# Loads in the order of need: keys' weights in halves, second attention's weights behind feed-forward chunks

## The chip, the cores and the metric

The kernel runs on one core of one Trainium2 chip. A core has a matrix engine (TensorE, PE in the profile), a vector engine (VectorE, DVE), an activation engine (ScalarE, ACT), a general engine (GpSimd, POOL) and a queue engine (SyncE, SP) that here only issues transfers. Data moves between the chip's memory and the core's SBUF by 16 DMA engines. The metric is the device time of one execution in microseconds, as the median of some runs.

## The reference, cut to what matters

Two layers, each a gated cross-attention and a gated feed-forward, over x of 2 x 2048 rows of 512 and a context of 2 x 128 rows of 384.

```
x = x + tanh(g_xattn[0]) * cross_attention_0(layernorm(x), ctx)     # 16 heads of 32, with biases
x = x + tanh(g_ffn[0])   * routed_block(layernorm(x))               # 256 rows of 2048 per batch:
                                                                    # causal attention, gated feed-forward 1365
x = x + tanh(g_xattn[1]) * cross_attention_1(layernorm(x), ctx)     # 16 heads of 64, inner width 1024
x = x + tanh(g_ffn[1])   * quantized_feed_forward(layernorm(x))     # 512 -> 2048, conv, silu, -> 512
```

A cross-attention needs keys = ctx @ Wk, values = ctx @ Wv, queries = x @ Wq, softmax over the 128 context rows, and an output projection with Wo and bo. The routed block scores all rows of a batch, takes the 256 highest, runs attention and a feed-forward on them and writes them back. The two matrices of the last feed-forward are first reduced to the values -1, 0, 1 (`ternary`).

## The kernel before, in words

Rows are worked in blocks of 512, four tiles of 128 rows by 512. The work has these stages.

- Opening (lines 986 to 1001): the weights of the first attention are loaded, the keys and values of the context computed (`keys_values`, line 176), and block 0 of x normalized, transposed and projected to queries (`front` and `queries` in `cross_attention`).
- First cross-attention, with the router and the first batch's selected attention fed in between its units (`beside`).
- First feed-forward on the selected rows of batch 0 (`feed_forward(0, ...)`, line 1033), with the rest of the router and the reduction of the second quantized matrix (`ternary(1, ...)`) in between.
- Selected attention of batch 1 with the second attention's keys and values in between (lines 1042 to 1061).
- Second feed-forward, batch 1 (line 1065), with `ternary(0, ...)` in between.
- Second cross-attention and the quantized feed-forward (from line 1077).

In names of the profile, `L_` stands for both `L0_` and `L1_`: L_ctxT, L_wk, L_wv, L_wq, L_wo, L_bo, L_bk, L_bq, L_bv are the context and the weights and biases of a cross-attention, L_kT and L_v its keys and values in SBUF. `pk` and `pv` are the PSUM tiles of keys and values (two buffers together in the opening), `xn` is a normalized tile of x, `ptr` its transpose, `pq` the queries. In the feed-forward, `w1c`, `w2c` and `w3c` are the weights of one chunk of 128 of the 1365 hidden columns (11 chunks, numbered 0 to 10, the last one of 85; three buffers each, loaded three chunks ahead), `pu` and `pw` the two up-projections, `gT` their gated product, `acc` the down-projection. `hn` is a normalized selected row tile, `wv` and `wqk` the selected attention's weights, `w_d` the quantized second matrix in memory, `w2b` its tile in SBUF, `xf` the x tiles of the second cross-attention.

A scheduler places every instruction on its engine. It keeps each engine's own order, adds the waits for data and for memory that is used again, and may move an instruction ahead of others that were written earlier if it is ready sooner. Each engine, and so each queue of transfers, then runs its instructions strictly in that order: an instruction that waits holds up all behind it. Nearly all transfers are issued on SP; in the opening ACT issues six and GpSimd two. In the built program each transfer on SP or ACT takes one of eight completion counters in turn, and waits until the transfer that had the counter before it has landed.

The weights of one attention are loaded by two methods. `load_context` issues the context, Wk, Wq, Wv and bv; `load_rest` issues Wo and bo and multiplies bo by the gate on VectorE. In the opening both are called at once. For the second attention `load_context` stands after the first feed-forward in the text and `load_rest` in the third step of the selected attention; the scheduler issues the first of them while the first feed-forward still loads its last chunks.

Of the kernel before, what the change touches and what calls it, by code (L numbers as in the profile page):

```python
# [17 lines left out]
P = 128  # L18
# [12 lines left out]
NF = (DFF + P - 1) // P  # L31
# [7 lines left out]
def row_tiles(ap):  # L39
    return ap.rearrange("(c p) n -> p c n", p=P)  # L40
# [3 lines left out]
def flamingo_kernel(ctx: ExitStack, tc: tile.TileContext, a: dict, out: bass.AP):  # L44
    nc = tc.nc
# [4 lines left out]
    def psum_pool(stack, name, bufs):  # L50
        return stack.enter_context(tc.tile_pool(name=name, bufs=bufs, space=PSUM))
# [23 lines left out]
    def in_pool(pool, tag):  # L75
        return lambda shape, name: pool.tile(shape, F32, name=name, tag=tag)
# [62 lines left out]
    class CrossWeights:  # L139


        def __init__(self, L, nE, bias, g, st, side):
            self.L, self.nE, self.bias, self.g = L, nE, bias, g
            E = nE * P
            w = st.enter_context(tc.tile_pool(name=L + "w", bufs=1, side=side))
            self.wq = w.tile([P, DC, E], F32, name=L + "wq")
            self.wo = w.tile([P, nE, D], F32, name=L + "wo")
            self.bo = w.tile([P, D], F32, name=L + "bo")
            self.kT = w.tile([P, B, nE, M], F32, name=L + "kT")
# [2 lines left out]
                self.bq = w.tile([P, nE], F32, name=L + "bq")  # L152
                self.bk = w.tile([P, nE], F32, name=L + "bk")

        def load_context(self, st, side):

            L, E = self.L, self.nE * P
            wkv = st.enter_context(tc.tile_pool(name=L + "wkv", bufs=1, side=side))
            self.ctxT = wkv.tile([P, CC, B * M], F32, name=L + "ctxT")
            nc.sync.dma_start(out=self.ctxT, in_=row_tiles(a["ctxT"]))  # L160
            self.wk = wkv.tile([P, CC, E], F32, name=L + "wk")
            nc.sync.dma_start(out=self.wk, in_=row_tiles(a[L + "WkT"]))
            nc.sync.dma_start(out=self.wq, in_=row_tiles(a[L + "WqT"]))
            self.wv = wkv.tile([P, CC, E], F32, name=L + "wv")
            nc.sync.dma_start(out=self.wv, in_=row_tiles(a[L + "WvT"]))
            if self.bias:
                self.bv = wkv.tile([P, E], F32, name=L + "bv")
                nc.sync.dma_start(out=self.bv, in_=a[L + "bv"].partition_broadcast(P))

        def load_rest(self):  # L170
            L = self.L
            nc.sync.dma_start(out=self.wo, in_=row_tiles(a[L + "WoT"]))
            nc.sync.dma_start(out=self.bo, in_=a[L + "bo"].partition_broadcast(P))
            nc.vector.tensor_scalar(self.bo, self.bo, self.g, None, ALU.mult)
# [432 lines left out]
        yield from rms_rows(rows, g2, h2T[b], mm, pool)  # L607

    AHEAD = 3

    def feed_forward(b, ps_acc, mm, work):

        w13, gT = {}, {}
        acc = [ps_acc.tile([P, D], F32, name=f"acc{i}", tag=f"acc{i}") for i in range(2)]

        def load(f):
            n = min(P, DFF - f * P)
            w1c = wst.tile([P, DC, P], F32, name="w1c", tag="w1c")
            nc.sync.dma_start(
                out=w1c[:, :, :n], in_=row_tiles(a["W1T"])[:, :, ds(f * P, n)]  # L620
            )
            w2c = wst.tile([P, DC, P], F32, name="w2c", tag="w2c")
            nc.sync.dma_start(
                out=w2c[:, :, :n], in_=row_tiles(a["W2T"])[:, :, ds(f * P, n)]
            )
            w3c = wst.tile([P, D], F32, name="w3c", tag="w3c")
            nc.sync.dma_start(out=w3c[:n, :], in_=a["W3T"][ds(f * P, n), :])
            w13[f] = (w1c, w2c, w3c)

        def down(f):  # L630
            n = min(P, DFF - f * P)
            for i in range(2):
                nc.tensor.matmul(
                    acc[i],
                    gT[f][:n, ts(i, P)],
                    w13[f][2][:n, :],
                    start=(f == 0),
                    stop=(f == NF - 1),
                )

        for f in range(AHEAD):
            load(f)
        for f in range(NF):
            n = min(P, DFF - f * P)
            pu, pw = mm([P, CAP], "pu"), mm([P, CAP], "pw")
            for pt, wt in ((pu, w13[f][0]), (pw, w13[f][1])):
                for d in range(DC):
                    nc.tensor.matmul(
                        pt[:n, :],
                        wt[:, d, :n],  # L650
                        h2T[b][:, d, :],
                        start=(d == 0),
                        stop=(d == DC - 1),
                    )
            su = fact.tile([P, CAP], F32, name="su", tag="su")
            nc.scalar.activation(su[:n, :], pu[:n, :], AF.Silu)
            gT[f] = fact.tile([P, CAP], F32, name="gT", tag="gT")
            nc.vector.tensor_tensor(gT[f][:n, :], pw[:n, :], su[:n, :], ALU.mult)
            if f > 0:
                down(f - 1)  # L660
                if f - 1 + AHEAD < NF:
                    load(f - 1 + AHEAD)
            for w, n in work:
                for _ in range(n):
                    next(w, None)
        down(NF - 1)
        for w, _ in work:
            for _ in w:
                pass

        for i in range(2):
            t = xa[2 * b + i]
            nc.vector.tensor_tensor(t, acc[i], t, ALU.add)
            nc.vector.tensor_scalar(t, t, gf[0], None, ALU.mult)
            nc.gpsimd.indirect_dma_start(
                out=x_d[b][:, :],
                out_offset=bass.IndirectOffsetOnAxis(
                    ap=idx[:, 2 * b + i : 2 * b + i + 1], axis=0
                ),
                in_=t,  # L680
                in_offset=None,
                compute_op=ALU.add,
            )
# [61 lines left out]
    with ExitStack() as st:  # L745
# [16 lines left out]
            out=pick,  # L762
            in_=pick,
# [10 lines left out]
            out=after,  # L774
            in_=after,
# [7 lines left out]
        def load_x(n, queue=nc.sync):  # L783
            if n < B * NBLK:
                for t in range(n * TB, (n + 1) * TB):
                    x[t] = xres.tile([P, D], F32, name="x", tag="x")
                    queue.dma_start(out=x[t], in_=x_in[t])
# [198 lines left out]
        sel_pools = selected_pools(st)  # L986
        W0 = CrossWeights("L0_", D // P, True, gx[0], st, "left")
        nc.scalar.dma_start(out=W0.bk, in_=a["L0_bk"])
        load_x(0, nc.scalar)
        nc.scalar.dma_start(out=W0.bq, in_=a["L0_bq"])  # L990
        with ExitStack() as st0:
            W0.load_context(st0, "left")
            W0.load_rest()
            nc.sync.dma_start(out=w_router, in_=a["w_router"].partition_broadcast(P))
            nc.vector.tensor_reduce(w_sum, w_router, AX.X, ALU.add)
            for n in (1, 2):
                load_x(n)
            selected_constants()
            with ExitStack() as st1:
                for _ in W0.keys_values(in_pool(psum_pool(st1, "L0_ps0", 2), "kv")):  # L1000
                    pass
# [18 lines left out]
    sf = ExitStack()  # L1020
    wst = sf.enter_context(tc.tile_pool(name="wst", bufs=AHEAD))
    fact = sf.enter_context(tc.tile_pool(name="act_ffn", bufs=3))
# [19 lines left out]
    right, right1, right2 = ExitStack(), ExitStack(), ExitStack()  # L1042
    w4 = right.enter_context(tc.tile_pool(name="w4", bufs=1, side="right"))
    w1q = w4.tile([P, DC, HID], BF16, name="w1q")
    W1 = CrossWeights("L1_", 1024 // P, False, gx[1], right1, "right")
    W1.load_context(right2, "right")
    with ExitStack() as sp:
        ps_o = psum_pool(sp, "s2b_o", 2)
        ps_sc = psum_pool(sp, "s2b_sc", 4)
        mm = in_pool(psum_pool(sp, "s2b_mm", 2), "mm")  # L1050
        second = selected_attention(
            1, mm, in_pool(ps_sc, "sc"), in_pool(ps_o, "o"), 4, selected_pools(sp), 2
        )
        keys_values = W1.keys_values(mm)
        for k, _ in enumerate(second):
            if k == 2:
                W1.load_rest()
            if k % 3 == 1:
                next(keys_values, None)
        for _ in keys_values:  # L1060
            pass
    with ExitStack() as sp:
        mm = in_pool(psum_pool(sp, "s2c_mm", 6), "mm")
        raw = raw_pools(sp)
        feed_forward(1, psum_pool(sp, "s2c_acc", 1), mm, [(ternary(0, mm, *raw), 1)])
    nc.vector.tensor_scalar(finstep, step[:, 1:2], gf[1], None, ALU.mult)
    sf.close()
    s2.close()
# [265 lines left out]
    def quantize_hidden(g):  # L1334
# [22 lines left out]

        AHEAD = 6
        hs = [load(c) for c in range(AHEAD)]
        s_b = scales_spread(g)  # L1360
# [155 lines left out]
```

## Time and profile before

| | us |
|---|---|
| median of 3 runs (1788.56 to 1795.08) | 1788.83 |
| the profiled execution | 1791.24 |
| its span | 1789.2 |

| engine | busy, us | share of the span |
|---|---|---|
| PE | 1647.3 | 92% |
| PE weight loads (beside PE) | 864.8 | 48% |
| DVE | 1250.1 | 70% |
| ACT | 1101.7 | 62% |
| POOL | 536.0 | 30% |

The mean granted clock of TensorE is 0.966 of full speed. The transfers move 196.99 MB, 110 GB/s over the span.

How to read the lines: times are microseconds from the start of the span. A line of the order in time gives start, length, engine, line of the code, operation, the tile written and the tiles read, the size and how many instructions were joined; in brackets is how long the engine stood idle before it, and what ended that. SPq, ACTq and POOLq are the queues' own issuing of transfers. A line of stretches gives the stretch, its length, the busy time of PE, its weight loads, DVE, ACT and POOL with the numbers of instructions, then the granted clock, the busy share of the DMA engines and GB/s. In the rows of 40 slices each digit is a busy share in tenths, for 44.7 us.

### The profile page before, as it was taken

The page shows a single profiled execution, that of the slowest core. Times are in us where ns is not written, and L with a number is a line of the kernel's source. Part 1 is how long each engine was busy: PE and PEld are TensorE (multiplying, and loading weights), DVE is VectorE, ACT ScalarE, POOL GpSimd, SP SyncE. Part 2 cuts the span into 40 slices and gives each one's busy share as a digit, 9 for nine tenths or more (in the row PEclk, how much of TensorE's full clock was granted, in tenths as well). Part 3 has the DMA queues.
Part 4 walks back from the last instruction along what each step waited for, and adds up shares of the span by engine and source line. Part 5 has one row for each costly group of instructions (what it writes and reads, how often), then busy time and mean ns, then how long its engine had stood idle before and what let it go on. Part 6 is the DMA issues. An engine that isn't in the chain of part 4 may idle for free.

```text
span 1789.2 us, 25277 instructions
## 1 busy us (share of the span) xinstructions
PE 1647.3 (92%) x8122; PEld 864.8 (48%) x8122; DVE 1250.1 (70%) x2544; ACT 1101.7 (62%) x3170; POOL 536.0 (30%) x671
## 2 busy tenths in 40 slices
PE   6999889899999889999999999999999999889968
PEld 3544444455555665755444544445454544434423
DVE  4566878865767443344378789897998789686956
ACT  2876566456553233345367778787787778744555
POOL 2534443342440011033134242432424224231100
PEclk9999999999999999999999999999999999899979
DMA  6011011121007861630012333233242233157374
GB/s 215 7 66 55 35 60 66 59 65 54 25 36 250 287 190 64 190 83 25 19 53 95 127 122 117 91 130 110 94 167 76 87 105 130 62 210 249 123 233 173
DMA packets 119828, 196.99 MB, mean 110 GB/s; under 512 B 12900, under 2 KB 50532, under 8 KB 115984
## 3 DMA queue, kind: packets, MB, share of 16 engines
q1 hardware_dynamic: 117872, 192.23, 31.5%
q0 software_dynamic: 960, 2.10, 0.6%
q8 instruction: 64, 1.05, 0.2%
q10 hardware_dynamic: 864, 1.05, 0.2%
q14 instruction: 68, 0.56, 0.1%
HBM read 120.89 MB, written 74.45 MB: 109 GB/s over the span
## 4 chain that ended last, share of the span: by engine, by line
PE 29%; DVE 15%; DMA 5%; ACT 4%; issue 2%; POOL 1%; SPq 1%; DVEq 0%; POOLq 0%; ACTq 0%
PE pq L253 8%; PE pp L320 8%; DVE h L1175 4%; PE po L302 3%; PE ph L1159 3%; PE sc L276 3%; PE po L1388 2%; PE tp L294 2%; DMA x<-h_d 1%; DVE u L1169 1%; DVE AT L295 1%; DVE nmx L119 1%; DMA hq<-hq_d 1%; DVE hf L1258 1%; DMA h_d<-h 1%
## 5 line engine op out<-in xcount | busy, mean ns | idle before, releaser
L122 ACT ACTIVATE A<-sc,nmx 128x128 f32<-128x128 f32 x1024 | 363.8, 385 | 131.5 <-DVE nmx L119 121.7
L131 POOL TENSOR_TENSOR A<-A,rden 128x512 f32<-128x512 f32 x256 | 275.9, 1079 | 506.7 <-DVE rden L130 410.8
L320 PE MATMUL pp<-L_wo,OT 128*128 128x512 f32 x768 | 366.8, 609 | 18.0 <-DVE x L329 11.9
L253 PE MATMUL pq<-xnT,L_wq 128*128 128x512 f32 x768 | 345.7, 598 | 12.2 <-DVE x L329 12.2
L122 ACT ACTIVATION_READ_ACCUMULATOR A<-sc,nmx 128x1 f32 x1024 | 229.7, 224 | 0.0
L253 PEld LDWEIGHTS pq<-xnT,L_wq 128*128 128x128 f32 x768 | 142.8, 191 | 172.1 <-issue 151.3
L119 DVE TENSOR_REDUCE nmx<-sc 128x4 f32<-128x512 f32 x256 | 168.6, 678 | 71.8 <-PE sc L276 71.6
L320 PEld LDWEIGHTS pp<-L_wo,OT 128*128 128x128 f32 x768 | 136.5, 193 | 164.4 <-issue 133.2
L1175 DVE SCALAR_TENSOR_TENSOR h<-u,cw,h 128x512 f32<-128x512 f32 x256 | 205.0, 834 | 6.0 <-ACT h L1171 5.5
L294 PE MATMUL tp<-ident,A 128*128 128x128 f32 x1024 | 164.4, 284 | 18.7 <-POOL A L131 13.2
L294 PEld LDWEIGHTS tp<-ident,A 128*128 128x128 f32 x1024 | 118.4, 143 | 87.6 <-issue 41.9
L295 DVE COPY AT<-tp 128x512 f32<-128x512 f32 x192 | 129.8, 678 | 43.5 <-PE tp L294 42.8
L276 PEld LDWEIGHTS sc<-L_kT,qT 32*128 32x128 f32 (+1 forms) x2048 | 110.6, 192 | 71.0 <-issue 58.5
L1388 PE MATMUL po<-w2q,hq 128*128 128x512 bf16 x512 | 122.2, 394 | 20.0 <-DVE hq L1370 9.0
L276 PE MATMUL sc<-L_kT,qT 32*128 32x128 f32 (+1 forms) x2048 | 137.0, 293 | 3.8 <-ACT A L122 3.2
L1171 ACT ACTIVATE h<-u,cb,cw 128x512 f32<-128x512 f32 x128 | 99.1, 808 | 64.7 <-DVE u L1169 53.6
L302 PE MATMUL po<-AT,L_v 128*32 128x512 f32 (+1 forms) x512 | 119.3, 657 | 11.7 <-DVE AT L295 11.1
L1159 PE MATMUL ph<-xiT,w1q 128*128 128x512 bf16 x512 | 124.3, 379 | 1.9 <-DVE u L1169 1.5
L1169 DVE TENSOR_TENSOR u<-ph,inv_b 128x512 f32<-128x512 f32 x128 | 84.9, 682 | 31.4 <-PE ph L1159 27.3
L130 DVE RECIPROCAL rden<-den 128x4 f32<-128x4 f32 x256 | 43.3, 169 | 80.0 <-ACT A L122 72.8
L1168 POOL COPY u<-carry 128x2 f32<-128x2 f32 x128 | 48.7, 382 | 167.3 <-DVE h L1175 141.3
L1170 POOL COPY carry<-u 128x2 f32<-128x2 f32 x128 | 49.8, 394 | 150.9 <-DVE u L1169 149.1
(238 smaller groups left out, 2362.6 us busy)
## 6 DMA issues: line engine op xcount, KB each, us to landing
h_d<-h SPq DMA_DIRECT2D x28, 1024.0 KB, 4.1
x_d<-x SPq DMA_DIRECT2D x64, 256.0 KB, 3.1
hf<-h_d SPq DMA_DIRECT2D x64, 256.0 KB, 3.4
x<-x_d SPq DMA_DIRECT2D x61, 256.0 KB, 4.7
x<-h_d SPq DMA_DIRECT2D x48, 256.0 KB, 5.5
x_d<-xo SPq DMA_DIRECT2D x32, 256.0 KB, 2.1
xf<-x_d SPq DMA_DIRECT2D x32, 256.0 KB, 3.6
hq_d<-hi SPq DMA_DIRECT2D x64, 128.0 KB, 1.8
```

The lines of the kernel that those rows point to most:

```text
L119: nc.vector.tensor_reduce(nmx, sc, AX.X, ALU.max, negate=True)
L122: nc.scalar.activation(out_tile[:, h, :], sc[:, h, :], AF.Exp, bias=nmx[:, h : h + 1], accum_out=den[:, h : h + 1],)
L131: nc.gpsimd.tensor_tensor(out_tile, out_tile, rden.unsqueeze(2).to_broadcast([P, n, width]), ALU.mult,)
L253: nc.tensor.matmul(pq, W.wq[:, d, ts(e, P)], xnT[:, d, :], start=(d == 0), stop=(d == DC - 1),)
L276: nc.tensor.matmul(sc[h][:, t, :], qT[e % cpg][r, ts(t, P)], W.kT[r, b, e, :], start=True, stop=True,)
L294: nc.tensor.transpose(tp[:, t, :], A[:, t, :], ident)
L295: copy(AT, tp.rearrange("p t n -> p (t n)"))
L302: nc.tensor.matmul(po[h * dh : (h + 1) * dh, :], W.v[:, b, ts(hd, dh)], AT[c * hpc + h], start=True, stop=True,)
L320: nc.tensor.matmul(pp, OT[e][:, ts(i, P)], W.wo[:, e, :], start=(e == 0), stop=(e == nE - 1),)
L1159: nc.tensor.matmul(ph, w1q[:, d, ts(c, P)], xiT[g][:, d, :], start=(d == 0), stop=(d == DC - 1),)
L1175: nc.vector.scalar_tensor_tensor(z, u[:, ds(k, BLK)], cw[:, c, k : k + 1], z, ALU.mult, ALU.add)
L1388: nc.tensor.matmul(po, rows(c), w2q[:, c, :], start=(c == 0), stop=(c == HC - 1))
```

## The change

`load_context` and `load_rest` become one generator, `load_keys`, in three steps: the context and Wk, the latter in two transfers of half the columns each; then Wv; then Wq, bv, Wo and bo with the multiplication of bo.

In the opening, the first two steps are issued, then the four tiles of x for block 0, which move from ACT's queue to SP's, then the third step.

For the second attention, the first step is queued on SP behind the load of w3c of chunk 9 of the first feed-forward, the second step (called at the first step of the selected attention) behind that of chunk 10, and the third step (called after the second feed-forward in the text) behind that of chunk 5 of the second feed-forward. `tc.issue_after` sets the order of issue only; nothing waits for the named transfer to land.

```diff
-        def load_context(self, st, side):
+        def load_keys(self, st, side):
 ...
             self.wk = wkv.tile([P, CC, E], F32, name=L + "wk")
-            nc.sync.dma_start(out=self.wk, in_=row_tiles(a[L + "WkT"]))
-            nc.sync.dma_start(out=self.wq, in_=row_tiles(a[L + "WqT"]))
+            for k in range(2):
+                half = ts(k, E // 2)
+                nc.sync.dma_start(
+                    out=self.wk[:, :, half], in_=row_tiles(a[L + "WkT"])[:, :, half]
+                )
+            yield
             self.wv = wkv.tile([P, CC, E], F32, name=L + "wv")
             nc.sync.dma_start(out=self.wv, in_=row_tiles(a[L + "WvT"]))
+            yield
+            nc.sync.dma_start(out=self.wq, in_=row_tiles(a[L + "WqT"]))
             if self.bias:
                 self.bv = wkv.tile([P, E], F32, name=L + "bv")
                 nc.sync.dma_start(out=self.bv, in_=a[L + "bv"].partition_broadcast(P))
-
-        def load_rest(self):
-            L = self.L
             nc.sync.dma_start(out=self.wo, in_=row_tiles(a[L + "WoT"]))
 ...
+    issued = {}
 ...
-            nc.sync.dma_start(out=w3c[:n, :], in_=a["W3T"][ds(f * P, n), :])
+            issued[b, f] = nc.sync.dma_start(out=w3c[:n, :], in_=a["W3T"][ds(f * P, n), :]).ins
 ...
-        load_x(0, nc.scalar)
         nc.scalar.dma_start(out=W0.bq, in_=a["L0_bq"])
         with ExitStack() as st0:
-            W0.load_context(st0, "left")
-            W0.load_rest()
+            loads = W0.load_keys(st0, "left")
+            next(loads)
+            next(loads)
+            load_x(0)
+            for _ in loads:
+                pass
 ...
-    W1.load_context(right2, "right")
+    loads = W1.load_keys(right2, "right")
+    with tc.issue_after(issued[0, NF - 2]):
+        next(loads)
 ...
-            if k == 2:
-                W1.load_rest()
+            if k == 0:
+                with tc.issue_after(issued[0, NF - 1]):
+                    next(loads)
 ...
+    with tc.issue_after(issued[1, 5]):
+        for _ in loads:
+            pass
```

In the built program the order of instructions on TensorE and GpSimd is the same but for the numbering of two small PSUM tiles. On SP the weights of chunks, the writes of w_d and the selected attention's weights around the moved loads stand in a somewhat different order. On VectorE and ScalarE the scheduler also changed the order in four places: in the opening the statistics of x stand between the evacuations of the keys; in the first feed-forward the reduction of the quantized matrix and `hn` stand ahead of the last products `gT`; the multiplication of the second attention's bo moves from the selected attention into the second feed-forward, between `gT` of chunks 8 and 9; and the statistics and normalization of the first `xf` tiles move to the end of that feed-forward.

## The prediction

> **What bounds the kernel now.** I read the page first (busy shares, slices), then the opening 45 us in order of time, the waits of SP's queue, TensorE's instructions in order of time around each light slice, and stretches with their granted clock.
>
> ```profile
> span 1789.2 us, 25277 instructions
> ...
> PE 1647.3 (92%) x8122; PEld 864.8 (48%) x8122; DVE 1250.1 (70%) x2544; ACT 1101.7 (62%) x3170; POOL 536.0 (30%) x671
> ...
> PE   6999889899999889999999999999999999889968
> ...
> DMA  6011011121007861630012333233242233157374
> ```
>
> TensorE is the bound: 92% busy. From 40 to 545 us it waits for other engines only, never for a load, so time won before 40 us is carried through. Two places show it waiting for a load: slice 1 (a 6) and the end of the first feed-forward, where DMA is at 7 to 8 tenths.
>
> ```profile
> 0.82 0.44 SPq L160 DMA_DIRECT2D L_ctxT<-in_ctxT  x1
> ...
> 1.31 0.48 SPq L162 DMA_DIRECT2D L_wk<-in_L_WkT  x1
> ...
> 1.85 0.48 SPq L163 DMA_DIRECT2D L_wq<-in_L_WqT  x1
> ...
> 11.58 8.19 PE L182 MATMUL pk<-L_ctxT,L_wk 128*128 128x256 f32 x24 [11.58 <-DMA L_wk<-in_L_WkT]
> ...
> 19.61 5.31 PE L201 MATMUL pv<-L_wv,L_ctxT 128*128 128x512 f32 x12
> ...
> 26.17 1.90 DVE L104 TENSOR_SCALAR xn<-x,L_ln_mv,L_ln_rstd 128x512 f32<-128x512 f32 x4
> ...
> 31.07 6.13 PE L253 MATMUL pq<-xnT,L_wq 128*128 128x512 f32 x10
> ```
>
> The first keys wait until 11.58 us for one 768 KB weight. The queries, first of the long work, start at 31.07: 3.0 us after the last xn ends (28.07).
>
> ```profile
> 6.00:7.00 1.00, 0.00 (x0) 0.00 (x0) 0.08 (x1) 0.00 (x0) 0.00 (x0) 1.00 1.14 341
> 7.00:8.00 1.00, 0.00 (x0) 0.00 (x0) 0.00 (x0) 0.00 (x0) 0.00 (x0) 1.00 0.68 66
> ...
> 9.00:10.00 1.00, 0.00 (x0) 0.00 (x0) 0.00 (x0) 0.00 (x0) 0.00 (x0) 1.00 0.51 82
> ```
>
> The last column is GB/s: 300 to 360 from 3 to 7 us, under 100 until 10, about 400 from 11 to 29. GpSimd's two small gate loads, issued at 1.61 and 2.40, land 7.6 and 9.1 us later, across that slump. The change leaves them, so I keep the slump.
>
> ```profile
> 609.18 0.45 SPq L163 DMA_DIRECT2D L_wq<-in_L_WqT  x1
> ...
> 611.86 0.35 SPq L627 DMA_DIRECT2D w3c<-in_W3T  x1
> ```
>
> ```profile
> 615.96 1.88 PE L633 MATMUL acc<-w3c,gT 128*128 128x512 f32 x4
> 622.11 3.75 PE L633 MATMUL acc<-w3c,gT 85*128 85x512 f32 x4 [4.27 <-DMA w3c<-in_W3T]
> 626.65 2.93 PE L182 MATMUL pk<-L_ctxT,L_wk 128*128 128x256 f32 x6 [0.78 <-DVE xa L673]
> ...
> 632.91 7.03 PE L484 MATMUL pv<-wv,hT 128*128 128x512 f32 x16
> ```
>
> ```profile
> 622.00:631.00 9.00, 8.11 (x18) 4.70 (x18) 3.31 (x7) 0.00 (x0) 1.68 (x1) 0.50 1.06 391
> ...
> 632.00:633.00 1.00, 1.00 (x6) 0.87 (x6) 0.20 (x1) 0.00 (x0) 0.00 (x0) 1.00 1.07 295
> ```
>
> The last down chunk, behind 2 MB of L_wq in SP's queue, makes TensorE stand 4.27 us; then the granted clock (third column from the end) is 0.50, until about 631.6.
>
> **The change, part by part.** The chip does the same arithmetic; each attention has one more DMA (keys' weights in two), at 0.48 us of SP's queue, hidden while SP waits.
>
> *Opening, transfers.* The ACT queue's four x loads (2.15 us of issuing; ACT then has nothing to run until 11.62) go to SP behind the values' weights. By the stretches, 0.58 MB have moved by 4 us, 0.89 by 5, 1.21 by 6, 1.79 by 10, 2.05 by 11, then 0.4 per us. In the new order ctxT and the first half make 0.79 MB (4.7 us), all keys 1.18 (5.9), values 1.97 (10.7), the x tiles 2.23, 2.49, 2.75 and 3.02 (11.4, 12.1, 12.7, 13.4). L_bo landed at 21.0 although its 5.64 MB were through at 19.9, so I add 1.1: half at 5.8, x tiles at 12.5, 13.2, 13.8, 14.5, L_bo at 21 as before, since the same bytes stand ahead of it. L_wq and bv, now behind x, come at 17.1 and 17.8, before the queries (27) and L_v (18.9) need them.
>
> *Opening, TensorE and VectorE.* The first keys start at 5.8, which alone would be 5.8 us won. But the built order of VectorE now puts the statistics of x between the evacuations L_kT, and keys and values share two PSUM buffers, so PE waits for x. Two key groups (12 records, at half clock 0.43 us each: 8.19 us for 24 fits 14 slow and 10 fast) end at 10.9, the third at 13.5. L_kT(1) comes after x0's statistics: 12.5 + 0.69 + 0.48 = 13.7; the fourth group ends by 16.2. L_kT(2), behind x1 and x2, ends at 15.6, L_kT(3), behind x3, at 16.9. Values: 16.2 + 5.3 = 21.5; L_v 0.69, three xn 1.43, L_bo 0.47 (landed at 21), one xn 0.5: 24.6 for 28.07. Gain 3.5. Without the slump x lands 2.5 earlier and PE sets the pace: 6. A second half as late as L_wk is now (11.46) gives about 2. I take 4.0, near the slump's row.
>
> A rule speaks against the halves: the Trainium skill, "DMA: Bandwidth & Descriptors", section Bandwidth, asks for transfers of 1 MiB and more, and its fit (2.0 us plus bytes over 436 GB/s) makes two 384 KB transfers 5.8 us where one of 768 KB takes 3.8. That would cut the opening to 2.0 us. The stretches from 3 to 7 us, 301 to 359 GB/s with transfers of 256 to 1024 KB in flight together, show the fixed part overlapped; I go by them.
>
> *After the opening* VectorE owes eight more statistics (0.86 each with their aggregate), w_sum 0.68 and four xn 1.9 before the first nmx: about 24.1 + 9.5 = 33.6, while the scores end 7.2 us after the queries start (38.3 - 31.07), at about 34.3. No loss; at a larger gain up to 1 us.
>
> *End of the first feed-forward.* L_wk, 1.5 MB, issued at 595.25 and L_wq at 609.18 leave the space ahead of the last chunk; ctxT (384 KB) and half the keys (768 KB) stay ahead of it. w3c's buffer comes free at 607.5; 1.2 MB plus 0.5 MB of quantized weights at 370 GB/s is 4.6 us: landed by 613.5 for a need at 617.84. VectorE's new order puts hn, which waits for the last w_d write, ahead of gT of chunks 9 and 10. Now those writes are late because of L_wk (VectorE stood 4.28 us for one at 605.42); without it (2.1 us to land) the last is issued at 607.6 and landed at 610, hn is done at 611, and gT(9) isn't needed until 615.96. So the wait goes: 4.27, plus acc 3.75 - 1.88 = 1.87, plus pk 2.93 - 1.46 = 1.47: 7.6 us. What is next is the selected rows' value weights, which now stand ahead of L_wv (that has until 674): 3.3 MB from 607.6 at 370 are there by 618.5 for pv at 632.91 - 7.6 = 625.3. The clock term is where a rule differs: "TensorE: Matmul & The Clock Gate", Part 1, has full clock after some 3.4 us of work, hence only 1.7 us lost and 6.0 in all; here the clock stays at half for 9.5 us of work, so I take 7.6.
>
> *Second feed-forward.* L_wq and L_wo (2 MB each, 5.4 us at 390) enter SP's queue after w1c(7) (issued at 727.65) and w1c(9) (738.2). Behind L_wq wait w3c(6), w2c(7), w1c(8): w2c(7) would land at about 738, need 743.2; behind L_wo w2c(9), about 748, need 753.5. L_bo now has VectorE wait in front of gT(9): landed about 752.5, need 755.3. The last two xf come behind w3c(10), issued at 752: xn of the next stage ends near 761.2 (now 755.5), gT(10) after it, need 762.3. All covered, by about 1 us at the last; I take 0.2 off. If that cover is gone, each late microsecond is one of PE's, plus a slow clock. L_wq is needed at 765.6, far off.
>
> Sum: 4.0 + 7.6 - 0.2 = 11.4 us. The profiled execution is 1791.24 us (span 1789.2 and 2.0 around it), 2.4 above the median of the runs, 1788.83; from its own time 1779.8, from the median **1777.4**.
>
> **The rivals.**
> - *Opening given back* (14%): keys start early, but values and xn wait for x as long as now. For it: the interleaving above. Gain 7.4: 1781.4.
> - *Tail stays late* (8%): the 1.2 MB ahead of w3c, or hn before gT, hold PE. Against it: 4 us of slack. Gain 3.8: 1785.
> - *Slower* (8%): L_wq and L_wo stall the second feed-forward as L_wq stalled the first, 7.6 us each: 1788.83 - 11.4 + 15.2 = 1792.6, more where the chunks behind stall too. It decides once w2c(7) takes over 11.7 us from issue; the stalled w3c took 10.2.
> - *More* (8%): the slump came of the x loads on a second queue and goes: opening 6 to 6.5, 1775 or, with 3 us of clock elsewhere, 1772.
>
> **How the numbers follow.** The forecast has 62%, its own range 1774 to 1780. About 0.5% (8.9 us) is what a measurement tells from none. Faster by more: 60 of these, 8 of "more", 5 of the first rival, 73%. Within: 2, 9, all 8 of the late tail, 3 of the slower, 22%. Slower by more: 5%. The range, 1770 to 1785, takes in both first rivals and leaves out the slower.
>
> **What would show it.** First pk near 5.8 us; the fourth pk group released by L_kT; pq at 27 (24.6 if the slump goes). No stand before the last acc, full clock there, pv about 7.6 us closer to it. No load among PE's waits between the first acc of the second feed-forward and its end. Wrong: w2c or w3c as PE's releaser there, or pq at 30 or later.

## The result, and the profile after

| | before | after |
|---|---|---|
| median, us | 1788.69 (1787.93 to 1795.08, 4 runs) | 1777.78 (1775.98 to 1783.06, 4 runs) |
| the profiled execution, its span | 1791.24, 1789.2 | 1783.06, 1781.1 |
| mean granted clock of TensorE in it | 0.966 | 0.966 |

The ratio is 0.9939, with a 95% interval of 0.9912 to 0.9967: 10.9 us faster by the medians. The profiled execution is the slowest of the four runs of after, so the two traces differ by only 8.2 us. Where the other 2.7 us are is a question of its own, taken up below.

The page of after: the span, TensorE's busy share, and the 40 slices of TensorE and of the transfers.

```profile
span 1781.1 us, 25238 instructions
...
PE 1645.2 (92%) x8076; PEld 863.1 (48%) x8122; DVE 1249.4 (70%) x2544; ACT 1101.5 (62%) x3170; POOL 536.4 (30%) x671
...
PE   7999889899899999999999999999999999888968
...
DMA  6011112111007833720112333233242233156465
```

The busy time is nearly what it was; the first slice rose from 6 to 7. The opening of after in order of time:

```profile
1.31 1.01 SPq L164 DMA_DIRECT2D L_wk<-in_L_WkT  x2
2.90 5.31 SPq L791 DMA_DIRECT2D x<-in_x  x4
6.08 6.61 PE L185 MATMUL pk<-L_ctxT,L_wk 128*128 128x256 f32 x18 [6.08 <-DMA L_wk<-in_L_WkT]
...
13.44 0.69 DVE L99 BATCH_NORM_STATS2 L_ln_st<-x 128x6 f32<-128x512 f32 x1 [3.80 <-DMA x<-in_x]
14.05 0.47 DVE L194 TENSOR_SCALAR L_kT<-pk,L_bk 128x256 f32<-128x256 f32 x1
...
14.57 1.56 PE L185 MATMUL pk<-L_ctxT,L_wk 128*128 128x256 f32 x6 [1.88 <-DVE L_kT L194]
...
16.22 5.42 PE L204 MATMUL pv<-L_wv,L_ctxT 128*128 128x512 f32 x12
...
24.23 0.54 DVE L104 TENSOR_SCALAR xn<-x,L_ln_mv,L_ln_rstd 128x512 f32<-128x512 f32 x1
...
27.77 6.44 PE L256 MATMUL pq<-xnT,L_wq 128*128 128x512 f32 x10
```

The keys start 5.5 us earlier (6.08 for 11.58), but 3.3 us are left at the queries (27.77 for 31.07). The missing 2.2 us can be followed in four lines: x lands late (13.44), an evacuation of the keys (their copy from PSUM to SBUF, `L_kT`) stands behind its statistics on VectorE (14.05), the fourth group of keys waits 1.88 us for that evacuation, and the values follow it.

The slump in the transfers is still there, as the stretches of after show (the last number is GB/s). It was under 100 from 7 to 10 us; in this trace it is 144 to 190 from 5 to 9, and in a second trace of the same kernel (further down) 202, 95, 98 and 189 there.

```profile
5.00:6.00 1.00, 0.00 (x0) 0.00 (x0) 0.00 (x0) 0.00 (x0) 0.09 (x1) 1.00 0.72 156
...
7.00:8.00 1.00, 1.00 (x4) 0.75 (x3) 0.00 (x0) 0.00 (x0) 0.00 (x0) 1.00 0.93 144
```

The end of the first feed-forward in after, on TensorE in order of time, and the granted clock there (third number from the end):

```profile
613.15 3.60 PE L637 MATMUL acc<-w3c,gT 128*128 128x512 f32 x8
617.79 1.56 PE L185 MATMUL pk<-L_ctxT,L_wk 128*128 128x256 f32 x6 [1.05 <-DVE xa L677]
...
622.22 7.03 PE L487 MATMUL pv<-wv,hT 128*128 128x512 f32 x16
```

```profile
617.00:622.00 5.00, 3.80 (x19) 3.03 (x20) 3.31 (x8) 0.00 (x0) 1.68 (x1) 1.00 1.06 400
```

The last two down chunks run back to back, at full clock. From the start of chunk 9's down products to that of `pv` it was 632.91 - 615.96 = 16.95 us; now it is 622.22 - 613.15 = 9.07: a gain of 7.88. SP's queue shows why (order of time): the last w3c has the context (at 601.38) and half of the keys' weights, but no query weights, in front of it.

```profile
605.56 0.43 SPq L164 DMA_DIRECT2D L_wk<-in_L_WkT  x1
606.08 0.43 SPq L631 DMA_DIRECT2D w3c<-in_W3T  x1
606.57 0.40 SPq L164 DMA_DIRECT2D L_wk<-in_L_WkT  x1
```

The one wait for a load among TensorE's waits from 690 to 800 us in after (total, times, longest), and then the end of the second feed-forward in order of time, VectorE first:

```profile
PE pu L652 <- DMA w1c<-in_W1T: 0.2, 1, 0.2
```

```profile
748.73 1.91 DVE L104 TENSOR_SCALAR xf<-xf,L_ln_mv,L_ln_rstd 128x512 f32<-128x512 f32 x4 [1.12 <-POOL L_ln_rstd L90]
750.56 0.42 DVE L662 TENSOR_TENSOR gT<-pw,su 85x256 f32<-85x256 f32 x1
```

```profile
749.25 3.76 PE L637 MATMUL acc<-w3c,gT 128*128 128x512 f32 x8
752.85 1.93 PE L113 MATMUL ptr<-ident,xf 128*128 128x128 f32 x16
754.62 7.13 PE L256 MATMUL pq<-xnT,L_wq 128*128 128x512 f32 x16
```

It is 0.2 us, where the same wait took 0.5 before. The last `gT` stands behind four `xf` normalizations and comes at 750.98, where the products that read it are next: the eight take 3.76 us where they took 3.60 before. From `pv` to the first queries of the second attention it is 132.40 us for 132.72 before.

### The profile page after: what moved, and what is told of

Read it like the earlier page. It is cut to its first block, busy times and chain, and to the rows that moved or that the text cites. A ratio compares the mean times of both kernels' runs of the same rounds, so it can differ in the third digit from the quotient of the medians.

```text
span 1781.1 us, 25238 instructions
## 1 busy us (share of the span) xinstructions
PE 1645.2 (92%) x8076; PEld 863.1 (48%) x8122; DVE 1249.4 (70%) x2544; ACT 1101.5 (62%) x3170; POOL 536.4 (30%) x671
## 4 chain that ended last, share of the span: by engine, by line
PE 51%; DVE 26%; ACT 9%; DMA 7%; issue 3%; POOL 2%; SPq 1%; DVEq 0%; POOLq 0%; ACTq 0%
PE pp L323 12%; PE pq L256 10%; PE po L305 4%; DVE h L1188 4%; ACT A L122 4%; PE tp L297 3%; PE sc L279 3%; DVE marks L866 3%; DVE nmx L119 3%; PE ph L1172 2%; PE pu L652 2%; PE po L1401 2%; PE pw L652 2%; PE acc L637 2%; DVE AT L298 2%
## 5 line engine op out<-in xcount | busy, mean ns | idle before, releaser
L256 PE MATMUL pq<-xnT,L_wq 128*128 128x512 f32 x768 | 349.5, 603 | 12.2 <-DVE x L332 12.2
```

The lines of the kernel that those rows point to most:

```text
L256: nc.tensor.matmul(pq, W.wq[:, d, ts(e, P)], xnT[:, d, :], start=(d == 0), stop=(d == DC - 1),)
```

## The experiments

My theory: the opening's gain is set by the evacuations that stand behind x's statistics and by two buffers, the tail's by what is ahead of the last w3c in SP's queue, and the second feed-forward is covered. The rivals: the opening's gain is given back before the end, the slump is made by the x loads on a second queue, not by the two gate loads, each transfer pays a price of its own, or the cover in the second feed-forward is wide. Each experiment is a variant of after, but for the first two, which are before with one half of the change. The place that each is about is read in its trace; its whole time says less, as the last part of this document shows.

### The opening alone

In before, the opening lines alone are changed; the second attention keeps `load_context` and `load_rest`.

```diff
-        load_x(0, nc.scalar)
         nc.scalar.dma_start(out=W0.bq, in_=a["L0_bq"])
         with ExitStack() as st0:
-            W0.load_context(st0, "left")
-            W0.load_rest()
+            loads = W0.load_keys(st0, "left")
+            next(loads)
+            next(loads)
+            load_x(0)
+            for _ in loads:
+                pass
```

> The opening of the changed kernel alone; the second attention's loads stay as in the kernel before. My theory (two separate gains, carried through until TensorE's clock shifts them): first keys at 6.1 us, the queries pq at 27.8 instead of 31.1, a gain of 2.8 to 3.3 us at 45 us, and the stand before the last acc of the first feed-forward is back with about 4.3 us and half clock behind it; in all 3 us faster, 1785.5. Rival (the opening's gain is swallowed by waits that don't move with it): pq early, but the gain at 600 us is under 1 us. Rival (all of the gain is one thing): no stand before the last acc here either.

Measured: 1784.65 us (1781.28 to 1788.68, 20 runs) beside 1789.79 (29 runs), ratio 0.9967 (0.9955 to 0.9978). The keys start at 6.98 (after, with the same opening, has 6.08) and the queries at 27.30. The stand at the end of the first feed-forward is as it was, in order of time:

```profile
621.08 3.75 PE L657 MATMUL acc<-w3c,gT 85*128 85x512 f32 x4 [4.14 <-DMA w3c<-in_W3T]
625.61 2.93 PE L206 MATMUL pk<-L_ctxT,L_wk 128*128 128x256 f32 x6 [0.78 <-DVE xa L697]
```

So the opening is worth some 6 us over many runs (0.33% of 1789, between 3.9 and 8.1), and the rival that it is given back before the end falls. This trace shows less: a gain of 3.8 at the queries and 0.9 at `pv` of the selected attention (631.99 for 632.91). Of the 2.9 us between, 1.8 went to more time at half clock; the last part takes that up. That the runs gain more than the queries is in part the clock's, 0.9678 on average for 0.9664 in before; the rest is open.

### The second attention's loads alone

Before's opening is kept, and the second attention's weights are issued in the new order.

```diff
-    W1.load_context(right2, "right")
+    loads = W1.load_keys(right2, "right")
+    with tc.issue_after(issued[0, NF - 2]):
+        next(loads)
...
-            if k == 2:
-                W1.load_rest()
+            if k == 0:
+                with tc.issue_after(issued[0, NF - 1]):
+                    next(loads)
...
+    with tc.issue_after(issued[1, 5]):
+        for _ in loads:
+            pass
```

> The opening of the kernel before; only the second attention's loads are in the new order. My theory: pq at 31.1 us as before, no stand before the last acc, the selected pv some 7.4 us closer to it, in all 7 to 8 us faster, 1781. Rival[...]: only 6 us closer. Rival (L_wq and L_wo stall the second feed-forward): a load appears among TensorE's waits between 700 and 765 us, gain under 4.

Measured: 1783.28 us (1778.89 to 1785.82, 10 runs), ratio 0.9960 (0.9945 to 0.9975). Order of time on TensorE:

```profile
617.42 3.60 PE L658 MATMUL acc<-w3c,gT 128*128 128x512 f32 x8
622.07 1.56 PE L206 MATMUL pk<-L_ctxT,L_wk 128*128 128x256 f32 x6 [1.05 <-DVE xa L698]
...
626.49 7.03 PE L508 MATMUL pv<-wv,hT 128*128 128x512 f32 x16
```

Again 9.07 us from chunk 9's down products to `pv`, a gain of 7.88 and not 6, with no help from the opening: this trace was 1.46 us late at that point (617.42 for 615.96) and is 6.42 early after it. The second feed-forward takes 132.70 us from `pv` to the queries, as before. One expectation missed: with before's opening the queries start at 29.98, not near 31.1. So 1.1 us there is within what two traces of one opening differ by. By their ratios the two halves add up to 5.9 + 7.2 = 13.1 us (by the medians, 5.1 + 6.5 = 11.7); the whole change measured 10.9 above and 0.9917 (14.8 us) beside another set of runs of before. The two are additive within their intervals.

### Six buffers for keys and values

```diff
-                for _ in W0.keys_values(in_pool(psum_pool(st1, "L0_ps0", 2), "kv")):
+                for _ in W0.keys_values(in_pool(psum_pool(st1, "L0_ps0", 6), "kv")):
```

> The changed kernel with six PSUM buffers for keys and values in the opening instead of two. My theory (the fourth key group and the values wait for x's statistics only because they need the buffer back): no wait of pk for L_kT, pv ends near 19.5 instead of 21.7, pq at 25.5 instead of 27.8. Rival (the transfers set the opening, L_wv or L_bo come too late): pq within 0.7 us of 27.8, with L_bo or L_wv named as the releaser.

Measured: one run, 1789.46 us (span 1786.5). Order of time on TensorE:

```profile
6.04 8.47 PE L185 MATMUL pk<-L_ctxT,L_wk 128*128 128x256 f32 x24 [6.04 <-DMA L_wk<-in_L_WkT]
...
25.80 6.28 PE L256 MATMUL pq<-xnT,L_wq 128*128 128x512 f32 x10
```

All four key groups run without a wait, and the queries start 2.0 us before those of after. This is nearly all of the 2.2 us that the early start of the keys lost on the way: the evacuation behind x, with two buffers. But the one whole run is slower than all four of after. Most of the loss lies far from the edit, in a stretch at half clock that after doesn't have: this trace is 0.2 us ahead of after at 754 us and 4.5 behind at the next transposes of `xf` (804.58 for 800.10). The stretch in this kernel, clock third from the end:

```profile
773.00:783.00 10.00, 9.26 (x29) 6.35 (x29) 4.42 (x10) 5.94 (x32) 2.88 (x4) 0.52 0.02 7
```

### The gate loads on another queue

```diff
-    nc.gpsimd.dma_start(out=graw[:, 0:2], in_=a["g_xattn"].partition_broadcast(P))
-    nc.gpsimd.dma_start(out=graw[:, 2:4], in_=a["g_ffn"].partition_broadcast(P))
+    nc.scalar.dma_start(out=graw[:, 0:2], in_=a["g_xattn"].partition_broadcast(P))
+    nc.scalar.dma_start(out=graw[:, 2:4], in_=a["g_ffn"].partition_broadcast(P))
```

> The changed kernel with the two gate loads issued first on ACT's queue instead of GpSimd's. If GpSimd's loads make the slump of the transfers from 5 to 9 us (144 to 190 GB/s), it is gone: 300 GB/s and more there, x0 lands near 11 instead of 13.4, pq near 25.6. If the slump has another cause (the narrow rows of the halves and of the biases), GB/s stays under 200 for some microseconds and pq within 0.7 of 27.8.

Measured: one run, 1775.13 us (span 1773.4). Two stretches of it:

```profile
5.00:6.00 1.00, 0.00 (x0) 0.00 (x0) 0.00 (x0) 0.00 (x0) 0.00 (x0) 1.00 0.47 145
6.00:7.00 1.00, 0.00 (x0) 0.00 (x0) 0.00 (x0) 0.68 (x1) 0.00 (x0) 1.00 1.05 347
```

The slump has moved: from 6 us on it is gone, but 2 to 6 us are slow instead (13, 162, 179 and 145 GB/s), until the second gate load has landed (`tanh`, which waits for it, is released at 6.32), and the keys start late, at 7.56. Even so, x's first statistics come at 11.41 for 13.44, no key group waits, and the queries start at 25.25. The next run moves the gate loads behind all that the keys need.

### The gate loads last, and six buffers

On top of the six buffers, the gate loads go on SP behind x, and `tanh` after them.

```diff
             load_x(0)
+            nc.sync.dma_start(out=graw[:, 0:2], in_=a["g_xattn"].partition_broadcast(P))
+            nc.sync.dma_start(out=graw[:, 2:4], in_=a["g_ffn"].partition_broadcast(P))
+            nc.scalar.activation(gate, graw, AF.Tanh)
```

> The changed kernel with six PSUM buffers for keys and values in the opening, and the two gate loads on SP's queue behind the x tiles of block 0. My theory: first keys at 5.5 to 6, no slump of the transfers before 10 us, no wait of pk for L_kT, pq near 24.4 instead of 27.8, 3.4 us won over the changed kernel; the median at about 1774, with the clock's half-speed stretches moving single runs by 3 us either way. Rival (the gain of the opening does not last to the end): pq near 24.4, but the median within 1 us of the changed kernel's.

Measured: 1777.08 us (1771.16 to 1784.37, 7 runs), ratio 0.9919 (0.9892 to 0.9947). Two stretches, then TensorE in order of time, then one line each of ScalarE and VectorE:

```profile
7.00:8.00 1.00, 1.00 (x4) 0.73 (x3) 0.00 (x0) 0.00 (x0) 0.00 (x0) 1.00 0.99 356
...
11.00:12.00 1.00, 1.00 (x7) 0.87 (x6) 1.00 (x4) 0.00 (x0) 0.00 (x0) 1.00 0.50 120
```

```profile
5.67 7.94 PE L182 MATMUL pk<-L_ctxT,L_wk 128*128 128x256 f32 x24 [5.67 <-DMA L_wk<-in_L_WkT]
...
21.40 2.01 PE L110 MATMUL ptr<-ident,xn 128*128 128x128 f32 x8 [2.63 <-DVE xn L101]
...
25.66 5.63 PE L253 MATMUL pq<-xnT,L_wq 128*128 128x512 f32 x10
```

```profile
16.14 1.28 ACT L998 ACT_TABLE_LOAD   x1 [16.14 <-DMA graw<-in_g_ffn]
...
19.37 1.29 DVE L210 TENSOR_TENSOR L_v<-pv,L_bv 128x512 f32<-128x512 f32 x2 [4.51 <-DMA L_bv<-in_L_bv]
```

No stretch from 3 to 11 us is under 292 GB/s. But the slump isn't gone: it follows the gate loads, which SP now issues at 5.08 and 5.66. From 11 us the transfers fall to 120 GB/s, stay at 252 to 307 until 17, and are back at 403 after that; `tanh` is released at 16.14. In all four kernels the full rate (347 GB/s and more) is back within a microsecond of the second gate load's landing, which is told by the release of `tanh`'s table load: back at 11, 10, 6 and 17 us, released at 11.62 in before, 10.61 in after, 6.32 with the gate loads on ACT and 16.14 here. So the two gate loads make it, whichever queue issues them. It isn't the x loads, which left ACT's queue in after while the slump stayed; and the two small loads of biases on ACT, issued by 1.7 us here, made none. Why two loads of 1 KB do this is not shown.

The moved slump has a price: bv, queued behind the gate loads, is late, VectorE stands 4.51 us for it with the values, the normalized tiles come behind, and `ptr` stands 2.63 us for `xn`. So the queries start 1.3 us later than expected.

### The changed kernel again, beside it

> The changed kernel itself, for more runs beside the one before on the same chip. The prediction's theory: 10 to 12 us faster than before, 1778; single runs spread by some 7 us. Rival (the first four runs fell well): under 8 us.

Measured: 1777.99 us (1775.33 to 1783.94, 6 runs), ratio 0.9917 (0.9887 to 0.9947). The queries start at 27.74; in this trace the second half of the keys' weights is late, which after's own trace doesn't show as a wait:

```profile
11.46 1.53 PE L185 MATMUL pk<-L_ctxT,L_wk 128*128 128x256 f32 x6 [0.74 <-DMA L_wk<-in_L_WkT]
15.15 1.56 PE L185 MATMUL pk<-L_ctxT,L_wk 128*128 128x256 f32 x6 [2.15 <-DVE L_kT L194]
```

The variant above starts its queries 2.1 us sooner, and its median is 0.9 us lower, with intervals that nearly coincide. Whether 2 us more in the opening reach the end, these medians can't tell.

### x back on ACT's queue

Everything else is as in after.

```diff
-            load_x(0)
+            load_x(0, nc.scalar)
```

> The changed kernel with the four x tiles of block 0 issued on ACT's queue again; the rest of the new order stays. The tiles share the transfers with the keys' and values' weights, and in the built order all of x's statistics stand ahead of the first L_kT. My theory (moving x behind the values is what lets the keys start, and x's statistics set the keys' pace): first keys 1 to 3 us later than 6.1, the third key group waits for the first L_kT until about 15, pq near 29 to 30. Rival (halving and reordering the weights alone does it): pq at 27.8 or earlier.

Measured: one run, 1779.26 us. Order of time on VectorE, then on TensorE:

```profile
11.03 0.69 DVE L99 BATCH_NORM_STATS2 L_ln_st<-x 128x6 f32<-128x512 f32 x1 [6.41 <-DMA x<-in_x]
...
15.62 0.48 DVE L194 TENSOR_SCALAR L_kT<-pk,L_bk 128x256 f32<-128x256 f32 x1
```

```profile
5.51 5.46 PE L185 MATMUL pk<-L_ctxT,L_wk 128*128 128x256 f32 x12 [5.51 <-DMA L_wk<-in_L_WkT]
16.15 5.33 PE L185 MATMUL pk<-L_ctxT,L_wk 128*128 128x256 f32 x12 [5.18 <-DVE L_kT L194]
```

One expectation missed: with x in flight beside their weights the keys start not later, but sooner. Then the scheduler puts all four statistics of x ahead of the first evacuation, TensorE stands 5.18 us, and the queries start at 32.16, later than before's 31.07 and than the 29 to 30 expected. So early keys by themselves are worth nothing here. By this trace the opening's gain rests on where x's statistics stand among the evacuations, and that followed from x's new place in the queue; this edit changes both and can't part them. The landing itself was not late: x's first statistics start 2.4 us before after's.

### The third step two chunks later

The remaining weights of the second attention, and the `xf` loads behind them, are issued behind chunk 8's w3c instead of chunk 5's.

```diff
-    with tc.issue_after(issued[1, 5]):
+    with tc.issue_after(issued[1, 8]):
```

> The changed kernel with L_wq, L_wo and L_bo queued behind w3c of chunk 8 of the second feed-forward instead of chunk 5. My theory (all is covered in the changed kernel, the last xf tiles by only about a microsecond): L_wq lands near 743, but the last three xf tiles and L_bo come behind L_wo, near 750; the transposes of xf that started at 752.9 start near 756 to 757, so TensorE stands 3 to 4 us, and the clock falls to half behind it; pq of the second attention 4 to 7 us later than 754.6. Rival (the cover is larger than I think): pq within 1 us of 754.6.

Measured: one run, 1793.44 us (span 1790.4). Order of time on TensorE:

```profile
760.71 3.67 PE L113 MATMUL ptr<-ident,xf 128*128 128x128 f32 x16 [5.02 <-DVE xf L104]
764.18 7.59 PE L256 MATMUL pq<-xnT,L_wq 128*128 128x512 f32 x16
```

From `pv` to the queries it is 764.18 - 625.54 = 138.64 us for after's 132.40: 6.2 more, in the expected 4 to 7, with a stand of 5.02 for the expected 3 to 4. The stand, and half clock after it (`ptr` takes 3.67 us for 1.93), are the price of `xf` being late; after has this cover, and no more than it needs.

### The keys' weights in one transfer

```diff
-            for k in range(2):
-                half = ts(k, E // 2)
-                nc.sync.dma_start(
-                    out=self.wk[:, :, half], in_=row_tiles(a[L + "WkT"])[:, :, half]
-                )
+            nc.sync.dma_start(out=self.wk, in_=row_tiles(a[L + "WkT"]))
```

> The keys' weights of both attentions are again loaded by one transfer each; everything else as after the change. By my working (bytes in flight together share the rate, and the evacuations behind x set the queries): the first keys start near 7 us instead of 6, when all 1.2 MB are there, the late second half (0.7 to 0.9 us of wait) is gone, and the queries stay within 0.3 us of the changed kernel's 27.8. By the rule that each transfer pays 2 us of its own (the Trainium skill, DMA: Bandwidth & Descriptors, Bandwidth): the keys complete and the x tiles land up to 2 us sooner, and the queries start near 25.8. The end of the first feed-forward shows no wait for w3c by either.

Measured: one run, 1780.72 us beside one run of before at 1783.42, both on another chip than the runs above. Order of time on TensorE:

```profile
6.96 6.68 PE L181 MATMUL pk<-L_ctxT,L_wk 128*128 128x256 f32 x18 [6.96 <-DMA L_wk<-in_L_WkT]
...
14.46 1.56 PE L181 MATMUL pk<-L_ctxT,L_wk 128*128 128x256 f32 x6 [0.82 <-DVE L_kT L190]
...
27.75 5.27 PE L252 MATMUL pq<-xnT,L_wq 128*128 128x512 f32 x10
```

The keys start 0.9 us later than in after, and the queries at the same time. At the queries the halves neither help nor cost in this trace. Two things are not settled by it. In the five traces with halves, x on SP and the gate loads on GpSimd the keys start at 5.73 to 6.98, so that the halves win 0.9 us there isn't shown. And x's first statistics start at 12.00, where those five have 13.44 to 14.38: that is what the rival of 2 us per transfer forecast for x, but it doesn't reach the queries, which by the rival were to start near 25.8. That fit (the Trainium skill, "DMA: Bandwidth & Descriptors", "Anatomy of one DMA") is stated for transfers that GpSimd issues; these are SP's. So the price of a transfer of its own stays open for the landing of x. The first feed-forward's end has no wait for w3c here either, so it is the order, not the halving, that frees it.

## Why the prediction was right, and where not

**Opening, transfers.** Predicted: first half at 5.8, x0 at 12.5. In the trace: 6.08, and 13.44, 0.9 late. The working kept the bytes of before's stretches, but the slump moved: it is earlier and longer, and in the first trace shallower. Keeping it was right: the runs with other gate loads show that it goes with these two loads, which the change leaves. With them moved the "more" rival's queries near 24.6 were nearly reached (25.25, and 25.66 with six buffers), though its reason, x on a second queue, fell.

**Opening, TensorE and VectorE.** The fourth key group was to end by 16.2, the values at 21.5, the last `xn` at 24.6. They end at 16.13, 21.64 and 24.77. That the first of these fits is luck, two misses that cancel: x came 0.9 later, and the fourth group took 1.56 us where 2.58 at half clock were worked. The mechanism, evacuations behind statistics with two buffers, is shown by the six buffers: no wait, and 2.0 us. The gain at the queries is 3.3, near the 3.5 worked (2.7 between the two halves' traces, 27.30 for 29.98); the step to 4.0 on top was not borne out at this place. Whole runs of the opening alone gave 3.9 to 8.1 us, which takes in 4.0.

**After the opening.** No loss was expected at the first `nmx`, and there is none: in after VectorE waits 1.40 us there for the scores, so a larger gain had that much room, too.

**End of the first feed-forward.** Predicted 7.6, measured 7.88, and within 0.01 of it in all seven kernels with the new order and the halved weights. The chunks' side came as worked: `hn`, now ahead of the last two `gT`, ends at 608.83, which is 611.6 on the scale of before, for the 611 worked, well ahead of its need, and the rival of a late tail fell. The parts: from chunk 9's down products to `pk`, 10.69 - 4.64 = 6.05 us, for the 4.27 + 1.87 = 6.14 predicted. From `pk` to `pv`, 6.26 - 4.43 = 1.83, for 1.47: I counted the half clock on `pk` alone, but before's `ptr` at 629.37 ran in it as well (1.91 us; 1.34 in after). The measurement also decides between the rule and the row: by full clock after some 3.4 us of work (the Trainium skill, "TensorE: Matmul & The Clock Gate", Part 1) the sum was 6.0; the stretch at half clock that the stand brought was worth more.

**Second feed-forward.** Predicted -0.2 with about 1 us of cover at the last `xf`. The last `xn` ends at 750.64, 761.2 on the scale of before less the 11.0 by which the trace is ahead there, so 0.4 us later than worked. The cover was just used up: the last eight down products take 0.16 us longer. Against that stands a load wait that is 0.3 us shorter, and in all the stretch is 0.3 us shorter, within what it varies by between kernels (131.4 to 132.7). The slower rival, a stall like the first feed-forward's, did not come: no w2c or w3c waits. That it was near is shown by the third step two chunks later, where `xf` is late and 6.2 us go.

**"Time won before 40 us is carried through."** The prediction argued this up to 545 us, and its sum takes it for the rest. A single trace need not bear it out: the sum has no term for TensorE's stretches at half clock, for which only the "more" rival grants 3 us. Up to the second attention's queries the trace of after does well: of the opening's 3.30 us 2.81 are left at chunk 9's down products, the tail adds 7.88 and the second feed-forward 0.32, which makes 11.01 us for the 11.4 predicted. At the end it is 8.0 ahead (the last `hq` starts at 1769.94 for 1777.93), though none of the moved loads comes after that point. One place where time goes can be seen instruction by instruction. In before the instruction `tp` at 1123.62 stands 9.87 us behind its counterpart in after (1113.75), and a few instructions on, at 1133.02, only 8.20 (1124.82). The stretches between, of before and of after:

```profile
1123.62:1133.02 9.40, 7.61 (x51) 4.11 (x49) 6.17 (x14) 5.61 (x22) 2.08 (x3) 0.82 0.34 108
```

```profile
1113.75:1124.82 11.07, 8.91 (x51) 4.25 (x49) 6.17 (x14) 5.85 (x23) 2.08 (x2) 0.69 0.29 92
```

The same 51 products had the clock at 0.82 before and at 0.69 in after, and took 1.67 us longer. Such stretches come at 141 us (0.50) and 902 us (0.57) as well, where before has 1.00; others are in before and not in after, as at 652 us.

How much that makes of single runs is seen when the variants are set side by side (profiled runs):

| kernel | queries of the opening | first queries of the second attention | mean clock | span |
|---|---|---|---|---|
| before | 31.07 | 765.63 | 0.966 | 1789.2 |
| the opening alone | 27.30 | 764.07 | 0.968 | 1786.5 |
| the second attention's loads alone | 29.98 | 759.19 | 0.970 | 1782.9 |
| after | 27.77 | 754.62 | 0.966 | 1781.1 |
| changed kernel again | 27.74 | 756.67 | 0.967 | 1781.7 |
| six buffers | 25.80 | 754.40 | 0.963 | 1786.5 |
| gates on ACT | 25.25 | 750.61 | 0.971 | 1773.4 |
| gates last, six buffers | 25.66 | 750.73 | 0.976 | 1769.5 |
| x on ACT | 32.16 | 754.25 | 0.970 | 1777.6 |

The opening's queries differ by 7 us, and the spans don't follow them: x back on ACT, with the latest queries of all, is ahead of after at the end. They follow the clock, in one and the same kernel too: of 29 runs of before the slowest took 1799.02 us at a mean clock of 0.962, the fastest 1785.17 at 0.968.

The traces let the clock be taken out. Add up, over windows of 1 us, one less the granted clock: that is roughly the time lost to half clock. From the opening's queries to chunk 9's down products the eleven traces take 580.9 to 588.4 us, 7.5 apart; less that loss they take 560.4 to 563.6. From the second attention's queries to the end, before takes 1023.6 us and after 1026.5, of which 27.4 and 30.7 are such loss: without it 996.1 and 995.8 (the other nine 996.2 to 998.5, but 1003.2 for gates last, six buffers). So the 3.0 us that after's trace loses there are the clock's; the work itself carries the lead through. In the first stretch the 3.2 us that remain between the traces are as much as the opening's gain, so for the opening the proof is not in a trace but in the 20 runs of it alone.

That the median came within 0.4 us of the 1777.4 forecast is in part luck: the interval of the ratio leaves 5.9 to 15.7 us for the gain, and beside the other runs of before it was 14.8. Why a stretch at half clock starts is open.

## What to carry to other kernels

When a load stalls the bound engine, look at what stands ahead of it in its queue, and cost the stall with the slow clock that follows it: here 4.3 us of wait were worth 7.9. An early start is worth only what the next engine's order and the buffers let through; of 5.5 us at the first keys 3.3 reached the queries, and with x's statistics in the wrong place none. Read each part of a change at its own place in the trace, and the whole only from many runs, since the clock moves single runs of this kernel by more than the opening is worth; where two traces must be compared, take out the time at half clock first.

## What was not expected of the hardware

- Two gate loads of 1 KB, broadcast to 128 partitions, slowed all transfers of the core until they had landed: 66 to 190 GB/s for 3 to 4 us from GpSimd's queue (before and after), 13 to 179 for 4 us as the first loads of ACT's, 120 to 307 for 6 us behind x on SP's. With them queued behind x, 292 to 408 were seen from 3 to 11 us.
- TensorE's clock went to half with no stand of over 1 us before it: 10 us at 0.52 from 773 us with six buffers, TensorE busy for 9.26 of them, where after has 1.00 over the same stretch.
